# Statistics of a convolution output: separate moments per tile, or sums over the mirrored sum and difference

## The chip, the cores and the metric

The kernel runs on one core of a Trainium2 chip. The metric is the device time in microseconds (us) of one execution, as the median of several runs. A core has five engines that run their own instruction queues in order and wait for each other by semaphores: PE (TensorE, matrix products into PSUM), DVE (VectorE, element-wise work and reductions), ACT (ScalarE, functions of one element with an optional sum over the row), POOL (GpSimd) and SP (which only issues DMA transfers here).

## The reference

The input x has 16 images of 16 channels of 256 x 256 fp32 values. Two layers follow each other, each of the form x + layer(groupnorm(x)). The first layer is a circular 3 x 3 convolution, which the reference writes as a product in the Fourier domain. The second is a Laplace layer (poles and residues in the Fourier domain). What matters here is the normalization between them, called `_gn`: 8 groups of two channels, and for each image and group one mean and one variance over 2 x 256 x 256 values.

```
def _gn(v, G=8, eps=1e-5):
    g = v.reshape(B_, G, C_ // G, H_, W_)
    m = jnp.mean(g, axis=(2, 3, 4), keepdims=True)
    s = jnp.var(g, axis=(2, 3, 4), keepdims=True)
    return ((g - m) / jnp.sqrt(s + eps)).reshape(v.shape)

x = x + _L0_conv_ref(_gn(x), L0_conv_weight)      # the result is v below
x = x + _L1_conv_ref(_gn(x), ...)                 # needs mean and variance of v
```

So every element of v, the output of the first layer, has to enter a sum and a sum of squares before the second layer can scale it.

## The kernel before, in words

The kernel has four stages one after the other: the convolution (up to about 626 us), the transform of the rows and columns (`fold`, `lines`, `columns`), the mixing of channels, and the way back. Only the first stage is touched.

**Tiling.** An image enters as two halves (tiles `xt`, loaded by SP in one DMA each), with 128 partitions that hold four groups r of 32: r = 0, 1 are rows from the top, r = 2, 3 the mirrored rows from the bottom, so that element (row, column) of a tile of r = 0, 1 has its mirror image at the same place of a tile of r = 2, 3. An image makes four units u; the stage has 64 units in all. A unit of one r is a PSUM bank of 128 x 512 values; six banks rotate (`pc`, bufs=6).

**Steps.** The stage is one loop over steps g = 0 to 386, `conv(g)` being the first thing of each. A unit takes six steps of 16 matmul calls (L249), two phases by three taps; r = 2, 3 run three steps behind r = 0, 1. With n = g mod 6, the banks of r = 0, 1 are full at n = 5 and those of r = 2, 3 at n = 2. At once ACT evicts them (L266) into SBUF tiles `vt`, adding the bias. Two steps later (the list `later`) DVE calls `mirror`: it adds the tiles of r = 0, 1 and r = 2, 3 into `vsum` (L231) and subtracts them in place (L232). One step on (the list `folded`) SP gets four stores into the DRAM array vD (L292). The pools set how far this runs ahead: four `vt` tiles, two `vsum` tiles.

**Statistics of v, before.** A unit has four tiles of 512 values per partition. For r = 0 DVE computes mean and variance with bn_stats (L268, into `vst`), two steps after the eviction. For r = 1, 2, 3 the eviction itself also leaves the sum over the row (`accum_out` into `sums`), and a Square on ACT with the bias -mu (L274, into a `junk` tile that nobody reads) leaves the sum of squares about mu, an estimate of the mean of the image. Once per image bn_aggr (L286, and L836 for the last image) joins the four bn_stats. `v_stats` joins both kinds of moments with weights 1 and 3; it runs once for the first 12 images inside the stage, and once for the last four at the start of the next stage.

**What else stands in the queues.** `x_stats(b)` computes the statistics of the input image b some 40 steps ahead: 16 bn_stats of 128 x 512 on DVE (L166), bn_aggr (L174), then small DVE pieces and matmuls of one column in turn (L178 on PE after L174; L186 to L188 on DVE; L178 again; L194; a square root on ACT at L195; L154 to L211; L178; L217 and L218). Every piece has a fixed step before the image begins (22, 17, 16, 14, 12, 9, 5 and 3 steps). The generators of `tables` add pieces of the second layer's tables every second and every fourth step: POOL arithmetic (L497 to L502, L516, L518, L575 to L599), DVE (L508 to L512, reciprocals at L431, L580, L597), ACT functions with table loads (L425, L426, L498, L514) and PE (L450, L612). The order on every engine is the order in which the loop issues (`manual_schedule`): an instruction that waits holds all that stand behind it on its engine.

Of the kernel before, what the change touches and what calls it, by code (L numbers as in the profile page):

```python
# [9 lines left out]
FP = mybir.dt.float32  # L10
AF = mybir.ActivationFunctionType
ALU = mybir.AluOpType
AX = mybir.AxisListType
# [3 lines left out]
B = 16  # L17
C = 16
N = 256
P = 128  # L20
# [4 lines left out]
def conv_then_laplace_kernel(ctx: ExitStack, tc: tile.TileContext, a: dict, out: bass.AP):  # L25
# [15 lines left out]
    nc = tc.nc  # L41
    x = a["x"]
# [45 lines left out]
    tp = ptab.enter_context(tc.tile_pool(name="tables", bufs=1))  # L88
# [70 lines left out]
    def x_stats(b):  # L159


        st = sp.tile([P, C, 6], FP, name="xst", tag="xst")

        def moments(j):
            r0 = 1 + 2 * (j % 8)
            nc.vector.bn_stats(st[:, j, :], halves[b][j // 8][:, r0 : r0 + 2, 1 : N + 1])  # L166

        for j in range(8):
            yield 38 - j, lambda: moments(j)
        for j in range(8, C):  # L170
            yield 30 - j // 2, lambda: moments(j)
        q = sp.tile([P, 12], FP, name="xq", tag="xq")
        mean, pvar, mu, d, e, var, sd, tmp, r, nb, bias = (q[:, j : j + 1] for j in range(11))
        yield 22, lambda: nc.vector.bn_aggr(q[:, 0:2], st)  # L174

        def spread(lhs, rhs):
            ps = pst.tile([P, 512], FP, name="ps_stat", tag="ps_stat")
            nc.tensor.matmul(ps[:, 0:1], lhsT=lhs, rhs=rhs, start=True, stop=True)  # L178
            return ps[:, 0:1]

        ps = []
        yield 17, lambda: ps.append(spread(g128, mean))

        def about_mean():

            nc.vector.tensor_copy(mu, ps[0])  # L186
            nc.vector.tensor_tensor(d, mean, mu, ALU.subtract)
            nc.vector.scalar_tensor_tensor(e, d, d, pvar, ALU.mult, ALU.add)  # L188

        yield 16, about_mean  # L190
        yield 14, lambda: ps.append(spread(g128, e))

        def root():
            nc.vector.tensor_scalar(var, ps[1], 1e-5, None, ALU.add)  # L194
            nc.scalar.activation(sd, var, AF.Sqrt)  # L195

        yield 12, root
        wc = sp.tile([P, 2, 3, 32], FP, name="wc", tag="wc")

        def conv_weights():  # L200
            newton(sd, var, tmp)
            nc.vector.reciprocal(r, sd)
            nc.vector.scalar_tensor_tensor(
                wc.rearrange("p h t m -> p (h t m)"),
                wband.rearrange("p h t m -> p (h t m)"),
                r,
                imask.rearrange("p h t m -> p (h t m)"),
                ALU.mult,
                ALU.add,
            )  # L210
            nc.vector.tensor_scalar(nb, mu, r, -1.0, ALU.mult, ALU.mult)  # L211

        yield 9, conv_weights
        yield 5, lambda: ps.append(spread(wsum.rearrange("p c m -> p (c m)"), nb))

        def biases():
            nc.vector.tensor_copy(bias, ps[2])  # L217
            nc.vector.tensor_scalar(shift[:, b : b + 1], mu, -1.0, None, ALU.mult)  # L218
            ready[b] = wc, bias

        yield 3, biases

    vst = tp.tile([P, B, 4, 6], FP, name="vst", tag="vst")
    sums = tp.tile([P, 2, B, 12], FP, name="sums", tag="sums")
    shift = tp.tile([P, B], FP, name="shift", tag="shift")

    def mirror(g, b, u, lo, hi):
        both = fp.tile([P, 2, 2, N], FP, name="vsum", tag="vsum")  # L230
        nc.vector.tensor_tensor(both, lo, hi, ALU.add)  # L231
        nc.vector.tensor_tensor(lo, lo, hi, ALU.subtract)  # L232
        folded.append((g + 3, b, u, (both, lo)))

    def conv(g):


        for c in range(4):
            for r in range(4):
                at = g if r < 2 else g - 3  # L240
                if not 0 <= at < 24 * B:
                    continue
                b, u, n = at // 24, at // 6 % 4, at % 6
                phase, tap = n // 3, n % 3
                if n == 0 and c == 0:
                    acc[r] = pc.tile([P, 2, N], FP, name="ps_conv", tag="ps_conv")
                q = 8 * (u % 2) + c + phase + (r < 2)
                rows = slice(32 * r, 32 * r + 32)
                nc.tensor.matmul(  # L249
                    acc[r][32 * c : 32 * c + 32],  # L250
                    lhsT=ready[b][0][rows, phase, tap],
                    rhs=halves[b][u // 2][rows, q : q + 5 : 4, 2 - tap : 2 - tap + N],
                    start=n == 0,
                    stop=n == 5,
                )
        for r in (0, 1) if g % 6 == 5 else (2, 3) if g % 6 == 2 else ():
            at = g if r < 2 else g - 3
            if not 0 <= at < 24 * B:
                continue
            b, u = at // 24, at // 6 % 4  # L260
            if r % 2 == 0:
                vt = vp.tile([P, 2, 2, N], FP, name="vt", tag="vt")
                acc["v", r // 2] = vt
            col = slice(3 * u + r - 1, 3 * u + r)
            by_sums = {"accum_out": sums[:, 0, b, col]} if r else {}
            nc.scalar.activation(vt[:, r % 2], acc[r], AF.Identity, bias=ready[b][1], **by_sums)  # L266
            if r == 0:
                later.append((g + 2, lambda b=b, u=u, v=vt[:, 0]: nc.vector.bn_stats(vst[:, b, u], v)))  # L268
            if r % 2 == 0:
                continue  # L270
            for k in (1,) if r == 1 else (2, 3):
                col = slice(3 * u + k - 1, 3 * u + k)
                junk = jp.tile([P, 2, N], FP, name="junk", tag="junk")
                nc.scalar.activation(  # L274
                    junk,
                    vt[:, k % 2],
                    AF.Square,
                    bias=shift[:, b : b + 1],
                    accum_out=sums[:, 1, b, col],
                )  # L280
            if r == 3:
                later.append((g + 2, lambda g=g, b=b, u=u, lo=acc["v", 0], hi=vt: mirror(g, b, u, lo, hi)))
        while later and (later[0][0] <= g or g >= 24 * B + 2):
            later.pop(0)[1]()
        if g % 24 == 4 and g >= 24:
            nc.vector.bn_aggr(ms[:, g // 24 - 1], vst[:, g // 24 - 1])  # L286
        while folded and (folded[0][0] <= g or g >= 24 * B + 2):
            _, b, u, tiles = folded.pop(0)
            for j, t in enumerate(tiles):
                for r in range(2):  # L290
                    y = 64 * r + 16 * u
                    nc.sync.dma_start(  # L292
                        out=vD[b][j, y : y + 16].rearrange("(t y) c x -> (y c) t x", t=2),
                        in_=t[:, r],
                    )

    ms = tp.tile([P, B, 2], FP, name="ms", tag="ms")
    vs = tp.tile([P, 6, B], FP, name="vs", tag="vs")
    vrhs = tp.tile([P, 2, B, C], FP, name="vrhs", tag="vrhs")

    def v_stats(b0, b1, bank):

        bs, nb = slice(b0, b1), b1 - b0
        n = 12.0 * 512
        m1, v1 = ms[:, bs, 0], ms[:, bs, 1]
        m2, v2, d, mean, mu, e = (vs[:, j, bs] for j in range(6))
        tt, ts, st = (
            nc.vector.tensor_tensor,
            nc.vector.tensor_scalar,
            nc.vector.scalar_tensor_tensor,  # L310
        )
        nc.vector.tensor_reduce(m2, sums[:, 0, bs], AX.X, ALU.add)
        nc.vector.tensor_reduce(v2, sums[:, 1, bs], AX.X, ALU.add)
        ts(m2, m2, 1 / n, None, ALU.mult)
        tt(d, m2, shift[:, bs], ALU.add)
        tt(d, d, d, ALU.mult)
        st(v2, v2, 1 / n, d, ALU.mult, ALU.subtract)
        st(mean, m2, 3.0, m1, ALU.mult, ALU.add)
        ts(mean, mean, 0.25, None, ALU.mult)
        yield  # L320
        ps = bank()[:, 0:nb]
        nc.tensor.matmul(ps, lhsT=g128, rhs=mean, start=True, stop=True)
        yield
        nc.vector.tensor_copy(mu, ps)
        for m, v in ((m1, v1), (m2, v2)):
            tt(d, m, mu, ALU.subtract)
            tt(d, d, d, ALU.mult)
            tt(v, v, d, ALU.add)
        st(e, v2, 3.0, v1, ALU.mult, ALU.add)
        ts(e, e, 0.25, None, ALU.mult)  # L330
        r = vrhs[:, :, bs]
        shape = [P, nb, C]
        for j, z in enumerate((mean, e)):
# [295 lines left out]
        for gen in gens:  # L629
            yield from gen  # L630

    ready, acc, later, folded = {}, {}, [], []
    for j, (_, piece) in enumerate(x_stats(0)):
        if j == 8:
            sum_taps()
# [13 lines left out]
    for g in range(24 * B + 3):  # L649
# [3 lines left out]
        b, n = divmod(g, 24)  # L653
# [179 lines left out]
    vq = fold(*units[0], loaded.pop(0))  # L833
    nc.vector.memset(sgn[:, 0:1], -1.0)
    nc.vector.memset(sgn[:, 1:2], 1.0)
    nc.vector.bn_aggr(ms[:, B - 1], vst[:, B - 1])  # L836
    rest = v_stats(B - 4, B, lambda: pa.tile([P, 512], FP, name="ps_y", tag="ps_y"))
    last = None
    for u in range(len(units) + 1):
# [46 lines left out]
    tp = pool(p2, "ct")  # L886
# [596 lines left out]
```

## Time and profile before

| | |
|---|---|
| runs | 2765.16, 2767.58, 2779.18 us; median 2767.58 us |
| profiled execution, first to last instruction | 2764.9 us |
| busy in the whole span | PE 2610.2, DVE 1916.6, ACT 1523.6, POOL 1062.1 us |
| first matmul and last matmul of the convolution | 26.2 and 625.1 us |
| bn_stats of v on DVE (L268) | 64 instructions, 42.9 us |
| Squares on ACT (L274) and their reads | 192 instructions, 138.3 us, and 36.3 us |
| sum (L231) and difference (L232) on DVE | 64 each, 81.0 and 89.0 us |

The profile is of one execution. A group's "busy" is the time covered by its instructions and "mean" the duration of one; two instructions of a pipelined engine can overlap, so a mean can be longer than the pace. "Idle before" is the time in which the engine stood still just before them, and the name after the arrow is what ended it. The chain of waits follows the work that ended last back to its beginning, at each step to what released it.

### The profile page before, as it was taken

To read this page: it belongs to the slowest core of one execution; us is meant where nothing else is said; L and a number is where in the kernel's file an instruction comes from. 1 tells how busy PE (TensorE), PEld (TensorE's weight loads), DVE (VectorE), ACT (ScalarE), POOL (GpSimd) and SP (SyncE) were. 2 spreads that over 40 slices of the span, in tenths; PEclk is the share of its full clock that TensorE was granted. 3 is DMA by queue.
4 is the path that set the end of the run, shared out by engine and by line. 5 is a ranking of instruction groups with operands and counts; after the bars stand their busy time and mean duration, and the time that the engine had idled before them with its cause. 6 is when DMAs were issued, how large, how long until landed. Compare 5 with 4: busy or idle time off the path is not lost.

```text
span 2764.9 us, 93061 instructions
## 1 busy us (share of the span) xinstructions
PE 2610.2 (94%) x39600; PEld 1959.1 (71%) x39600; DVE 1916.6 (69%) x3574; ACT 1523.6 (55%) x3092; POOL 1062.1 (38%) x989
## 2 busy tenths in 40 slices
PE   6888798898999999998999999999989999999998
PEld 3344344456777777776788888888778888888887
DVE  7788799977888888886444444444346667676766
ACT  4667687775666666664455555555434444444443
POOL 1334475612333333334111111111175656565653
PEclk9999999899999999999999999999999999999999
DMA  8778687755566555664666666666699989999995
GB/s 304 250 259 270 221 304 272 252 202 178 207 244 229 213 207 206 244 244 150 194 191 195 189 195 188 197 192 193 201 291 289 288 286 288 288 288 284 288 285 181
DMA packets 481199, 652.82 MB, mean 236 GB/s; under 512 B 51384, under 2 KB 459960, under 8 KB 466832
## 3 DMA queue, kind: packets, MB, share of 16 engines
q1 hardware_dynamic: 479712, 639.65, 71.2%
q8 instruction: 312, 5.11, 0.7%
q0 software_dynamic: 928, 3.02, 0.4%
q10 hardware_dynamic: 144, 4.19, 0.4%
q14 instruction: 103, 0.84, 0.1%
HBM read 367.22 MB, written 279.50 MB: 234 GB/s over the span
## 4 chain that ended last, share of the span: by engine, by line
PE 65%; DVE 13%; DMA 9%; POOL 4%; issue 4%; ACT 2%; SPq 2%; DVEq 0%; ACTq 0%; POOLq 0%
PE ps_mix L1055 16%; PE ps_s L989 9%; PE ps_y L737 8%; PE ps_y L745 8%; PE ps_conv L249 4%; PE ps_x L780 4%; DMA yk<-yD 4%; PE ps_p L1239 4%; PE ps_f L1263 4%; PE ps_f L1264 4%; DMA out_y<-ol 3%; DVE r L1272 2%; DVE xst L166 2%; PE psd L765 1%; DVE ol L1274 1%
## 5 line engine op out<-in xcount | busy, mean ns | idle before, releaser
L1055 PEld LDWEIGHTS ps_mix<-abd,sg 128*64 128x64 f32 x8192 | 447.6, 138 | 59.9 <-ACT sg L1112 48.9
L1055 PE MATMUL ps_mix<-abd,sg 128*64 128x128 f32 x8192 | 478.5, 275 | 7.8 <-ACT yt L1117 7.8
L249 PE MATMUL ps_conv<-xt,wc 32*32 32x512 f32 x12288 | 456.5, 622 | 17.7 <-issue 11.3
L1203 POOL TENSOR_TENSOR u<-yk 128x512 f32<-128x512 f32 (+1 forms) x268 | 343.9, 1314 | 311.0 <-PE ps_p L1239 204.2
L753 ACT ACTIVATE t<-ps_y,vmr 128x384 f32<-128x384 f32 x512 | 297.6, 582 | 163.0 <-PE ps_y L745 162.9
L249 PEld LDWEIGHTS ps_conv<-xt,wc 32*32 32x32 f32 x12288 | 233.0, 105 | 191.3 <-issue 111.9
L1117 DVE COPY yt<-ps_mix 128x512 f32<-128x512 f32 x128 | 88.5, 692 | 357.3 <-PE ps_mix L1055 234.0
L960 POOL TENSOR_TENSOR w<-v,mcol 128x2048 f32<-128x2048 f32 x32 | 115.6, 3612 | 561.5 <-DVE v L949 540.8
L737 PE MATMUL ps_y<-tabE,vq 128*128 128x256 f32 x1024 | 313.7, 388 | 8.7 <-DVE vq L726 7.1
L745 PE MATMUL ps_y<-tabO,vq 128*128 128x256 f32 x1024 | 306.4, 381 | 0.0
L1263 PE MATMUL ps_f<-pt,inv 128*128 128x256 f32 x1008 | 300.4, 380 | 0.0
L1264 PE MATMUL ps_f<-hs,ey 128*128 128x256 f32 x1008 | 299.8, 379 | 0.0
L1117 ACT COPY yt<-ps_mix 128x512 f32<-128x512 f32 x384 | 219.8, 588 | 144.7 <-PE ps_mix L1055 88.2
L1239 PEld LDWEIGHTS ps_p<-inv,u 128*128 128x128 f32 x2048 | 266.1, 193 | 43.2 <-issue 24.7
L1239 PE MATMUL ps_p<-inv,u 128*128 128x128 f32 x2048 | 279.4, 280 | 6.6 <-POOL u L1207 6.5
L1267 DVE TENSOR_TENSOR r<-ps_f,q 128x256 f32<-128x256 f32 x256 | 107.3, 419 | 248.9 <-ACT q L1266 248.9
L989 PE MATMUL ps_s<-ct,w 64*32 64x256 f32 x8448 | 261.0, 381 | 13.1 <-POOL w L957 12.2
L1112 ACT COPY sg<-ps_s 128x512 f32<-128x512 f32 x248 | 159.7, 645 | 190.4 <-PE ps_s L989 190.2
L1266 ACT COPY q<-ps_f 128x256 f32<-128x256 f32 x256 | 95.4, 373 | 285.4 <-PE ps_f L1264 283.1
L737 PEld LDWEIGHTS ps_y<-tabE,vq 128*128 128x128 f32 x1024 | 189.9, 191 | 85.3 <-ACT q L793 50.3
L266 ACT ACTIVATE vt<-ps_conv,xq 128x512 f32<-128x512 f32 x256 | 167.1, 680 | 137.7 <-PE ps_conv L249 135.9
L1241 ACT COPY pt<-ps_p 128x512 f32<-128x512 f32 x256 | 150.2, 587 | 132.4 <-PE ps_p L1239 118.7
(240 smaller groups left out, 4156.9 us busy)
## 6 DMA issues: line engine op xcount, KB each, us to landing
xt<-in_x SPq DMA_DIRECT2D x31, 2322.0 KB, 9.3
abd<-aD SPq DMA_DIRECT2D x512, 128.0 KB, 2.8
yD<-yt SPq DMA_DIRECT2D x512, 128.0 KB, 2.4
vl<-vD SPq DMA_DIRECT2D x256, 256.0 KB, 4.0
out_y<-ol SPq DMA_DIRECT2D x128, 512.0 KB, 9.4
s<-vD SPq DMA_DIRECT2D x252, 256.0 KB, 6.5
aD<-spec SPq DMA_DIRECT2D x15, 4096.0 KB, 12.6
yk<-yD SPq DMA_DIRECT2D x60, 1024.0 KB, 8.5
```

Of the source, the lines that this page charges most:

```text
L249: nc.tensor.matmul(acc[r][32 * c : 32 * c + 32], lhsT=ready[b][0][rows, phase, tap], rhs=halves[b][u // 2][rows, q : q + 5 : 4, 2 - tap : ...
L266: nc.scalar.activation(vt[:, r % 2], acc[r], AF.Identity, bias=ready[b][1], **by_sums)
L737: nc.tensor.matmul(ps[:, 0:N], lhsT=vf[:, xo, 0, j], rhs=tabE[:, 0 : i + 2 : i + 1], start=True, stop=False, skip_group_check=True,)
L745: nc.tensor.matmul(ps[:, P : P + N], lhsT=vf[:, xo, 1, j], rhs=tabO[:, i : C + 1 : C - i], start=False, stop=True, skip_group_check=True,)
L753: nc.scalar.activation(t[:, xo, j].rearrange("p l n -> p (l n)"), ps[:, 0:384], AF.Copy, scale=vmr[:, 0, b0 + j, i : i + 1],)
L989: nc.tensor.matmul(ps[odd][32 * iq : 32 * iq + 32, ro], lhsT=w[rows, iq, kk, ro], rhs=ct[rows, iq, kk], start=True, stop=True,)
L1055: nc.tensor.matmul(ps[64 * t : 64 * t + 64, j], lhsT=sg[:, f : f + 2].rearrange("p f m -> p (f m)"), rhs=abd[jq][:, :, 2 * t + cc, 2 * jj ...
L1117: (nc.vector.tensor_copy if m == 3 else nc.scalar.copy)(o, src)
L1203: nc.gpsimd.tensor_tensor(u[:, :, j].rearrange("p b (c n) -> p c b n", c=8), in0, in1, o)
L1239: nc.tensor.matmul(ps[:, at], lhsT=u[:, n], rhs=tab, start=True, stop=True)
L1263: nc.tensor.matmul(ps[:, e], lhsT=tab, rhs=pt[:, e], start=True, stop=False)
L1264: nc.tensor.matmul(ps[:, e], lhsT=ey[:, e], rhs=hs, start=False, stop=True)
```

## The change

The statistics of v are taken from the two mirrored tiles in place of the four tiles before. With a + b the sum and a - b the difference of mirrored values, the row sum of a + b is the sum of all values, and (a + b - 2 mu)^2 + (a - b)^2 is twice (a - mu)^2 + (b - mu)^2.

- The add of `mirror` becomes a scalar_tensor_tensor (lo x 1 + hi) with an accumulator output, on DVE.
- ACT squares `vsum` with the bias -2 mu, 1024 elements, one step after the stores are issued, and the difference without bias one step later, both with an accumulator output. A new list `squared` holds them; they come after `later` and before `folded` in a step.
- The bn_stats and bn_aggr of v, the accumulator outputs of the evictions and the Squares of 512 elements are gone.
- `biases` computes -2 mu too; `v_stats` has one kind of moments and fewer small instructions; `junk` grows from 512 to 1024 elements.

```diff
@@ x_stats, biases
             nc.vector.tensor_scalar(shift[:, b : b + 1], mu, -1.0, None, ALU.mult)
+            nc.vector.tensor_scalar(shift2[:, b : b + 1], mu, -2.0, None, ALU.mult)
...
     def mirror(g, b, u, lo, hi):
         both = fp.tile([P, 2, 2, N], FP, name="vsum", tag="vsum")
-        nc.vector.tensor_tensor(both, lo, hi, ALU.add)
+        nc.vector.scalar_tensor_tensor(
+            both, lo, 1.0, hi, ALU.mult, ALU.add, accum_out=sums[:, b, u : u + 1]
+        )
         nc.vector.tensor_tensor(lo, lo, hi, ALU.subtract)
         folded.append((g + 3, b, u, (both, lo)))
+        squared.append((g + 4, lambda: square(both, 4 + 2 * u, b, bias=shift2[:, b : b + 1])))
+        squared.append((g + 5, lambda: square(lo, 5 + 2 * u, b)))
+
+    def square(t, col, b, **by):
+
+        junk = jp.tile([P, 4 * N], FP, name="junk", tag="junk")
+        nc.scalar.activation(
+            junk,
+            t.rearrange("p r j x -> p (r j x)"),
+            AF.Square,
+            accum_out=sums[:, b, col : col + 1],
+            **by,
+        )
...
@@ conv
-            col = slice(3 * u + r - 1, 3 * u + r)
-            by_sums = {"accum_out": sums[:, 0, b, col]} if r else {}
-            nc.scalar.activation(vt[:, r % 2], acc[r], AF.Identity, bias=ready[b][1], **by_sums)
-            if r == 0:
-                later.append((g + 2, lambda b=b, u=u, v=vt[:, 0]: nc.vector.bn_stats(vst[:, b, u], v)))
-            if r % 2 == 0:
-                continue
-            for k in (1,) if r == 1 else (2, 3):
-                col = slice(3 * u + k - 1, 3 * u + k)
-                junk = jp.tile([P, 2, N], FP, name="junk", tag="junk")
-                nc.scalar.activation(
-                    junk,
-                    vt[:, k % 2],
-                    AF.Square,
-                    bias=shift[:, b : b + 1],
-                    accum_out=sums[:, 1, b, col],
-                )
+            nc.scalar.activation(vt[:, r % 2], acc[r], AF.Identity, bias=ready[b][1])
             if r == 3:
                 later.append((g + 2, lambda g=g, b=b, u=u, lo=acc["v", 0], hi=vt: mirror(g, b, u, lo, hi)))
...
-        if g % 24 == 4 and g >= 24:
-            nc.vector.bn_aggr(ms[:, g // 24 - 1], vst[:, g // 24 - 1])
+        while squared and (squared[0][0] <= g or g >= 24 * B + 2):
+            squared.pop(0)[1]()
...
@@ v_stats
-        nc.vector.tensor_reduce(m2, sums[:, 0, bs], AX.X, ALU.add)
-        nc.vector.tensor_reduce(v2, sums[:, 1, bs], AX.X, ALU.add)
...
-        st(mean, m2, 3.0, m1, ALU.mult, ALU.add)
-        ts(mean, mean, 0.25, None, ALU.mult)
+        nc.vector.tensor_reduce(mean, sums[:, bs, 0:4], AX.X, ALU.add)
+        nc.vector.tensor_reduce(v2, sums[:, bs, 4:12], AX.X, ALU.add)
...
+        st(v2, v2, 0.5 / n, d, ALU.mult, ALU.subtract)
...
-        for m, v in ((m1, v1), (m2, v2)):
-            tt(d, m, mu, ALU.subtract)
-            tt(d, d, d, ALU.mult)
-            tt(v, v, d, ALU.add)
-        st(e, v2, 3.0, v1, ALU.mult, ALU.add)
-        ts(e, e, 0.25, None, ALU.mult)
+        tt(d, mean, mu, ALU.subtract)
+        tt(d, d, d, ALU.mult)
+        tt(e, v2, d, ALU.add)
...
-    nc.vector.bn_aggr(ms[:, B - 1], vst[:, B - 1])
```

More of the change, by code (lines that the diff above doesn't have):

```diff
@@ L218, in biases @@
             nc.vector.tensor_scalar(shift[:, b : b + 1], mu, -1.0, None, ALU.mult)
+            nc.vector.tensor_scalar(shift2[:, b : b + 1], mu, -2.0, None, ALU.mult)
             ready[b] = wc, bias
         yield 3, biases
-    vst = tp.tile([P, B, 4, 6], FP, name="vst", tag="vst")
-    sums = tp.tile([P, 2, B, 12], FP, name="sums", tag="sums")
+    sums = tp.tile([P, B, 12], FP, name="sums", tag="sums")
     shift = tp.tile([P, B], FP, name="shift", tag="shift")
+    shift2 = tp.tile([P, B], FP, name="shift2", tag="shift2")
     def mirror(g, b, u, lo, hi):
         both = fp.tile([P, 2, 2, N], FP, name="vsum", tag="vsum")
-        nc.vector.tensor_tensor(both, lo, hi, ALU.add)
+        nc.vector.scalar_tensor_tensor(
+            both, lo, 1.0, hi, ALU.mult, ALU.add, accum_out=sums[:, b, u : u + 1]
+        )
         nc.vector.tensor_tensor(lo, lo, hi, ALU.subtract)
         folded.append((g + 3, b, u, (both, lo)))
+        squared.append((g + 4, lambda: square(both, 4 + 2 * u, b, bias=shift2[:, b : b + 1])))
[9 more added lines that the diff above has]
+        )
     def conv(g):
@@ L295, in conv @@
                     )
-    ms = tp.tile([P, B, 2], FP, name="ms", tag="ms")
-    vs = tp.tile([P, 6, B], FP, name="vs", tag="vs")
+    vs = tp.tile([P, 5, B], FP, name="vs", tag="vs")
     vrhs = tp.tile([P, 2, B, C], FP, name="vrhs", tag="vrhs")
@@ L303, in v_stats @@
         bs, nb = slice(b0, b1), b1 - b0
-        n = 12.0 * 512
-        m1, v1 = ms[:, bs, 0], ms[:, bs, 1]
-        m2, v2, d, mean, mu, e = (vs[:, j, bs] for j in range(6))
+        n = 16.0 * 512
+        v2, d, mean, mu, e = (vs[:, j, bs] for j in range(5))
         tt, ts, st = (
@@ L311, in v_stats @@
         )
-        nc.vector.tensor_reduce(m2, sums[:, 0, bs], AX.X, ALU.add)
-        nc.vector.tensor_reduce(v2, sums[:, 1, bs], AX.X, ALU.add)
-        ts(m2, m2, 1 / n, None, ALU.mult)
-        tt(d, m2, shift[:, bs], ALU.add)
+        nc.vector.tensor_reduce(mean, sums[:, bs, 0:4], AX.X, ALU.add)
+        nc.vector.tensor_reduce(v2, sums[:, bs, 4:12], AX.X, ALU.add)
+        ts(mean, mean, 1 / n, None, ALU.mult)
+        tt(d, mean, shift[:, bs], ALU.add)
         tt(d, d, d, ALU.mult)
-        st(v2, v2, 1 / n, d, ALU.mult, ALU.subtract)
-        st(mean, m2, 3.0, m1, ALU.mult, ALU.add)
-        ts(mean, mean, 0.25, None, ALU.mult)
+        st(v2, v2, 0.5 / n, d, ALU.mult, ALU.subtract)
         yield
@@ L630, in chain @@
             yield from gen
-    ready, acc, later, folded = {}, {}, [], []
+    ready, acc, later, folded, squared = {}, {}, [], [], []
     for j, (_, piece) in enumerate(x_stats(0)):
```

## The prediction

> **What bounds the kernel now.** I read the windows first, to see which stretch of the span the change can touch. The columns are the window, then busy us and instruction count of PE, PEld, DVE, ACT and POOL, then the TensorE clock and the DMA.
>
> ```profile
> core 0: us, PE busy (x) PEld busy (x) DVE busy (x) ACT busy (x) POOL busy (x), PEclk, DMA share, GB/s
> 0.00:26.00 26.00, 1.52 (x6) 1.35 (x6) 13.90 (x37) 1.49 (x2) 0.19 (x4) 1.00 0.86 333
> 26.00:200.00 174.00, 148.93 (x3338) 72.84 (x3337) 142.36 (x252) 117.16 (x260) 61.60 (x49) 0.93 0.79 265
> 200.00:350.00 150.00, 126.04 (x2956) 62.20 (x2956) 123.30 (x208) 104.05 (x232) 67.67 (x57) 0.96 0.71 244
> 350.00:500.00 150.00, 135.13 (x3549) 69.11 (x3527) 143.06 (x221) 125.09 (x297) 97.34 (x101) 0.98 0.82 292
> 500.00:600.00 100.00, 86.29 (x2160) 45.14 (x2156) 88.56 (x172) 66.94 (x165) 38.65 (x43) 0.91 0.60 215
> 600.00:626.00 26.00, 25.72 (x760) 17.80 (x741) 12.43 (x13) 20.99 (x55) 3.17 (x4) 1.00 0.66 223
> ```
>
> The convolution runs from 26 to 626 us. DVE is busy 142.4 + 123.3 + 143.1 + 88.6 + 12.4 = 510 of those 600 us, PE 522, ACT 434. From 350 to 500 DVE is full (95%). Before that neither PE nor DVE is: they wait for each other. After 600 PE alone sets the pace: the last units follow each other every 6.2 us, against 600/64 = 9.4 us on average.
>
> Next, who waits for whom inside that stretch (us, times, longest), and the groups of DVE and of ACT that the change touches, from 0 to 640 us (busy us, mean ns, idle before and who ended it):
>
> ```profile
> ACT vt L266 <- PE ps_conv L249: 135.9, 58, 12.1
> ...
> DVE vsum L231 <- ACT vt L266: 31.5, 14, 3.3
> ...
> PE ps_stat L178 <- DVE xq L188: 26.1, 9, 6.6
> PEld ps_conv L249 <- ACT vt L266: 19.4, 24, 5.9
> ```
>
> ```profile
> L232 DVE TENSOR_TENSOR vt<-vt 128x1024 f32<-128x1024 f32 x64 | 89.0, 1390 | 2.2
> L231 DVE TENSOR_TENSOR vsum<-vt 128x1024 f32<-128x1024 f32 x64 | 81.0, 1265 | 34.2 <-ACT vt L266 34.2
> L268 DVE BATCH_NORM_STATS2 vst<-vt 128x6 f32<-128x512 f32 x64 | 42.9, 670 | 5.9 <-ACT vt L266 5.9
> ...
> L286 DVE BATCH_NORM_AGGREGATE ms<-vst 128x2 f32<-128x24 f32 x15 | 3.8, 252 | 0.0
> ```
>
> ```profile
> L266 ACT ACTIVATE vt<-ps_conv,xq 128x512 f32<-128x512 f32 x256 | 167.1, 680 | 137.7 <-PE ps_conv L249 135.9
> L274 ACT ACTIVATE junk<-vt,shift 128x512 f32<-128x512 f32 x192 | 138.3, 720 | 4.2
> L266 ACT ACTIVATION_READ_ACCUMULATOR vt<-ps_conv,xq 128x1 f32 x192 | 37.7, 197 | 0.0
> L274 ACT ACTIVATION_READ_ACCUMULATOR junk<-vt,shift 128x1 f32 x192 | 36.3, 189 | 0.0
> ```
>
> PE's largest wait is for the statistics of the next image (xq, L188), which DVE delivers late because other work stands ahead of them in its queue. ACT has slack: it waits 136 us for PE. So a DVE instruction less is worth something, an ACT instruction less little. The chain of waits from 26 to 626 us, added up piece by piece, has 177 us of DVE, 160 of PE, 94 of POOL, 60 of ACT, 22 of DMA and 86 of "issue". On it lie 21 of the 64 vst instructions (12.4 us), 22 of the vsum ones (27.3 us), 4 of ms (0.7 us), and 37.6 us of evictions and squares (L266 26.4, L274 11.2).
>
> **What the Trainium skill says.** "ScalarE: Activation LUTs", What ACT_TABLE_LOAD costs: an ACTIVATE takes about 186 ns + 0.833 ns per element, 93 ns more with a per-partition bias. The trace agrees: L274, with bias, 720 ns for 512; L425 with a per-partition operand 714 and L426 without 620. "VectorE: DVE Perf Modes", Two Vector instructions with no wait between them: an op that also writes its accumulator is two instructions, the second an accumulator read. The trace of before shows no such DVE op; on ACT the pair is there (L266, L274). "Vector Engine (DVE) Microarchitecture Reference", Points that are easy to get wrong: a scalar_tensor_tensor with two non-bf16 SBUF sources halves throughput, with no port left for accumulator readback. Without accumulator the trace disagrees: L1272, two fp32 SBUF sources, takes 2321 ns for 2048, the rate of a tensor_tensor (1219 ns for 1024 in L729). With one, no row shows it.
>
> **The change part by part.**
>
> 1. DVE, removed: 64 vst at 670 ns = 42.9 us, 16 ms at 0.25 us = 4.1 us. Both stand in the in-order queue in front of the xq pieces: at image step 24b-17 a vst comes directly ahead of L186 to L188. On the chain: -12.4 - 0.7 = -13.1 us.
> 2. DVE, the sum becomes a scalar_tensor_tensor with accumulator. The element rate is that of L1272, so the main part stays at 1218 ns. Unknown is the accumulator read. Lower bound: nearly nothing, as on ACT, where in back-to-back pairs the read lengthens the pace by 0.10 us though it lasts 0.19. Upper bound: half rate. From L725 (512 elements, 693 ns) to L729 (1024, 1219 ns) an element costs 1.03 ns, so 1024 more are 1.05 us. A cost below zero is excluded: same elements, one write more. I take 0.15 us, a small DVE instruction (L186 lasts 0.14). 64 x 0.15 = 9.6 us of work, 22 x 0.15 = +3.3 us on the chain. Its two SBUF inputs are those of the old add, so nothing changes against POOL.
> 3. DVE, one shift2 per image: 16 x 0.142 (L218) = 2.3 us, times DVE's share of the chain (177/600) = +0.7 us. v_stats loses 7 small instructions per call (0.17 to 0.6 us each); one call lies behind the chain's xq pieces at 504 us, the other is on the chain at 642 us: -1 us in all.
> 4. ACT, per unit before: four evictions at a pace of 0.575 us, three reads at 0.095, three squares at 0.84 with read = 5.1 us. After: four evictions 2.3; a square of 1024 with bias 720 + 512 x 0.833 = 1146 ns and one without 1053 ns, each with 0.12 for the read: 2.44; 4.74 in all. Saving 7% of ACT's 37.6 us on the chain: -2.7 us. Evictions also end 0.1 to 0.2 us earlier. There is no change in table loads (47 either way).
> 5. ACT, the new wait. The squares of unit k stand behind the evictions of r 0, 1 of unit k+1 and wait for DVE's sum and difference; queued behind them are the evictions of r 2, 3 of unit k+1, and the square roots and table pieces of the other generators. Unit by unit: the difference (L232) ends a median 0.3 us after those evictions, but 3 us or more in 15 units. With 0.5 us less DVE lag and 1.17 us of square after it, the next eviction would start later than now in 35 units, more than 2.2 us later in 5. PE needs the bank three steps (3.5 us) after it was filled and the pair takes 1.27 us to evict, so 2.2 us are covered by the six banks; the 5 units exceed this by 5.9 us together. Half of that was PE waiting anyway: +3 us. What is late next there is the eviction, then PE's first matmul of the next r 2, 3 group.
> 6. DMA: the same four stores per unit at the same step on SP's queue. The tiles are freed by the stores; the squares, one and two steps after the issue, end about when the store lands (2.1 to 9 us after its issue). Nothing: the next user of a vsum buffer is the sum two units, 12 steps, later; only with that cover gone would a square (1.2 us) hold DVE or an eviction.
> 7. "Issue" pieces of the chain hide a stretch (434 to 482 us, 28 us) in which POOL waits for ACT, and ACT for DVE at full load: 28 x (35 us saved of 510) = -2 us.
>
> Sum: -13.1 + 3.3 + 0.7 - 1 - 2.7 + 3 - 2 = -11.8 us. The profiled span of 2764.9 us becomes 2753; it stands 2.7 us under the median of the runs shown, 2767.6, which becomes 2756. The removed pieces bound the gain of this one chain; PE and POOL chains lie close behind it, so I count no second-order gain.
>
> **The rivals.** *DVE is the bound everywhere:* then all of its saving counts, 42.9 + 4.1 - 9.6 - 2.3 = 35 us, less the PE-bound tail: about 30 us, 2737. For it: 95% from 350 to 500. Against it: 82% before that, and 48 us in which DVE waits for ACT (L231, L268, xq L174).
>
> *Another path takes over:* the POOL chain of the tables (94 us on the chain, L497 to L502 ahead of L508) or the new wait of step 5 in full (+6) eat the gain: 2763 to 2768. For it: PE, DVE, ACT and POOL take turns on the chain. Against it: the vst sits in front of the very xq pieces that PE waits for longest.
>
> *Slower, the accumulator at half rate:* the sum takes 2.3 us instead of 1.22. On the chain 22 x 1.05 = 23 us instead of 3.3 gives +8; by DVE's total, 64 x 1.05 = 67 against 45 us removed, +22, and the mirror's delay lands on the ACT squares of step 5 as well. 2775 to 2795, say 2784. It decides from 0.7 us of extra per sum (45 us/64). For it: the skill's sentence. Against it: L1272 shows no halving. *The change doing less than it says* is no case: the instruction lists show vst, ms and the 192 small squares gone.
>
> **How the numbers follow.** A measurement of this kernel can tell about 0.5% (14 us) from no change. The forecast (5 to 20 us faster) has 0.45, of which 0.2 is beyond 14 us; DVE as the bound everywhere 0.13; another path takes over (within 5 us) 0.24; half rate 0.18, all but 0.01 slower by over 14 us if counted with a bad case of step 5. That gives 0.33 faster, 0.50 within, 0.17 slower. The likeliest time is 2756 (own range 2747 to 2763); the range that takes in the others is 2735 to 2785.
>
> **What would show it.** Right: vsum at 1.2 to 1.3 us with a read of 0.1 to 0.2, squares at about 1.15 and 1.05 us, the stretch from 26 to 626 us some 10 us shorter, the PE wait for xq L188 below 26 us, and a new ACT wait for vsum or vt of some tens of us that PE hardly feels. Wrong: vsum at 2.3 us (half rate); PE waits for vt well over 20 us (step 5 too small); or an unchanged stage end with more POOL and PE on the chain.

## The result and the profile after

Twelve runs of each kernel gave medians of 2761.8 us (after) and 2772.1 us (before). The ratio of all runs is 0.9965, with a 95% interval of 0.995 to 0.998: about 10 us faster (6 to 14). That is less than the half per cent at which the prediction put the limit of what can be told, but the interval leaves out 1. A second measurement of the same kernel, in the last group of experiments, gave 0.9953 (0.9938 to 0.9969), 13 us. The median of before is here 4.5 us above that of the three runs that the prediction started from (2767.6), so it is the difference that can be compared with the forecast, not the 2756 us.

The profile of after is of the fastest of its twelve executions (2749.86 us). The profile of its second measurement is of the slowest of six (2765.85 us); in it the stage ends at 614.5 us and PE waits 12.5 us for xq L188. What the two traces of one kernel differ by (609.2 against 614.5 us, 10.1 against 12.5 us) is what a single trace can't tell.

The windows of the kernel after, in the columns of the prediction's first fence:

```profile
26.00:200.00 174.00, 150.99 (x3437) 73.47 (x3437) 139.65 (x258) 114.02 (x181) 63.46 (x51) 0.93 0.82 273
200.00:350.00 150.00, 133.90 (x3061) 61.22 (x3061) 117.12 (x215) 101.52 (x168) 73.71 (x65) 0.98 0.76 254
350.00:500.00 150.00, 139.53 (x3560) 67.19 (x3554) 137.98 (x239) 118.80 (x204) 97.04 (x97) 1.00 0.83 290
500.00:600.00 100.00, 90.43 (x2459) 51.31 (x2459) 73.14 (x144) 69.26 (x125) 37.03 (x41) 0.97 0.63 220
```

PE does more in every window: 150.99 against 148.93, 133.90 against 126.04, 139.53 against 135.13, 90.43 against 86.29. The last convolution matmul ends at 609.2 us instead of 625.7. The whole stage, in the kernel before and then in the kernel after:

```profile
26.00:625.70 599.70, 522.09 (x12704) 267.10 (x12703) 509.71 (x863) 433.96 (x1006) 268.43 (x252) 0.95 0.74 256
26.00:609.00 583.00, 523.84 (x12703) 258.44 (x12703) 471.05 (x856) 410.03 (x686) 271.69 (x252) 0.97 0.78 263
```

What gets shorter is the idle time of PE, from 77.6 to 59.2 us. The granted clock rises with the change, from 0.95 to 0.97, but PE's busy time does not fall (522 and 524 us), so the gain does not show as faster matmuls. Added up over the convolution, DVE's busy time falls by 38.7 us (509.7 to 471.1) but the stage by 16.5, so most of what DVE saves turns into idle time of DVE: 90 us of it before, 112 after.

The waits of the kernel after inside the stage (us in total, times, longest):

```profile
ACT vt L280 <- PE ps_conv L265: 114.8, 59, 11.1
...
DVE vsum L232 <- ACT vt L280: 47.0, 24, 4.1
ACT junk L243 <- DVE vsum L232: 43.0, 17, 7.3
...
PEld ps_conv L265 <- ACT vt L280: 25.8, 30, 6.8
...
PE ps_stat L178 <- DVE xq L188: 10.1, 4, 5.8
...
PE ps_conv L265 <- ACT vt L280: 8.8, 8, 5.8
```

PE's wait for evictions on the matmuls, in before:

```profile
PE ps_conv L249 <- ACT vt L266: 6.3, 4, 5.0
```

This is the trade. PE's wait for the next image's statistics (xq L188) falls from 26.1 to 10.1 us. The new wait, ACT for DVE's sum, is there with 43 us. PE's waits for evictions grow (19.4 to 25.8 on the weight loads, 6.3 to 8.8 on the matmuls), and DVE waits more for evictions (31.5 to 47.0).

The touched groups of DVE and of ACT (busy, mean ns, idle before):

```profile
L235 DVE TENSOR_TENSOR vt<-vt 128x1024 f32<-128x1024 f32 x64 | 89.3, 1395 | 2.2
L232 DVE SCALAR_TENSOR_TENSOR vsum<-vt 128x1024 f32<-128x1024 f32 x64 | 80.4, 1256 | 51.8 <-ACT vt L280 47.0 <-DMA s<-vD 4.8
...
L232 DVE DVE_READ_ACCUMULATOR vsum<-vt 128x1 f32 x64 | 5.1, 80 | 0.0
```

```profile
L280 ACT ACTIVATE vt<-ps_conv,xq 128x512 f32<-128x512 f32 x256 | 160.3, 681 | 115.3 <-PE ps_conv L265 114.8
L243 ACT ACTIVATE junk<-vsum,shift 128x1024 f32<-128x1024 f32 x64 | 73.3, 1146 | 43.3 <-DVE vsum L232 43.0
L243 ACT ACTIVATE junk<-vt 128x1024 f32<-128x1024 f32 x64 | 67.7, 1057 | 4.4 <-DVE vt L235 2.9
```

The sum with accumulator runs at the rate of the plain add (1256 against 1265 ns), and its read takes 80 ns. The squares are as worked out (1146 and 1057 ns). Where the new wait stands in the queue shows in the timeline of one unit (start, duration, what):

```profile
141.13 1.26 ACT L280 ACTIVATE vt<-ps_conv,xq 128x512 f32<-128x512 f32 x2 [2.02 <-PE ps_conv L265]
...
143.04 1.22 DVE L232 SCALAR_TENSOR_TENSOR vsum<-vt 128x1024 f32<-128x1024 f32 x1
144.18 0.08 DVE L232 DVE_READ_ACCUMULATOR vsum<-vt 128x1 f32 x1
...
144.30 1.23 DVE L235 TENSOR_TENSOR vt<-vt 128x1024 f32<-128x1024 f32 x1
144.30 1.15 ACT L243 ACTIVATE junk<-vsum,shift 128x1024 f32<-128x1024 f32 x1 [1.90 <-DVE vsum L232]
...
145.62 1.06 ACT L243 ACTIVATE junk<-vt 128x1024 f32<-128x1024 f32 x1
...
146.68 1.24 ACT L280 ACTIVATE vt<-ps_conv,xq 128x512 f32<-128x512 f32 x2
```

The accumulator read begins before the sum has ended, and the difference starts 1.26 us after the sum, where the plain add of before took 1.24 (407.51 to 408.75 us in its trace). Over all 64 units the medians of this step are 1.27 and 1.25 us. ACT, after the evictions at 141.13, stands still for 1.9 us; the next evictions start at once after the second square, with no idle time in front: what they needed was there before ACT came to them.

### The profile page after: what moved, and what is told of

The parts are those of the page before. It is cut to its first block, busy times and chain, and to the rows that moved or that the text cites. A ratio compares the mean times of both kernels' runs of the same rounds, so it can differ in the third digit from the quotient of the medians.

```text
span 2748.0 us, 92740 instructions
## 1 busy us (share of the span) xinstructions
PE 2611.5 (95%) x39600; PEld 1950.7 (71%) x39600; DVE 1875.8 (68%) x3560; ACT 1497.9 (55%) x2772; POOL 1068.9 (39%) x989
## 4 chain that ended last, share of the span: by engine, by line
PE 68%; DVE 11%; DMA 8%; POOL 5%; issue 4%; ACT 2%; SPq 2%; DVEq 0%; ACTq 0%; POOLq 0%
PE ps_mix L1047 16%; PE ps_s L981 9%; PE ps_y L730 9%; PE ps_y L738 8%; PE ps_p L1231 5%; PE ps_f L1255 4%; PE ps_x L773 4%; PE ps_f L1256 4%; PE ps_conv L265 4%; DMA yk<-yD 4%; DVE r L1264 2%; DVE xst L166 2%; DMA out_y<-ol 2%; PE psd L758 1%; PE ps_h L1215 1%
## 5 line engine op out<-in xcount | busy, mean ns | idle before, releaser
L265 PE MATMUL ps_conv<-xt,wc 32*32 32x512 f32 x12288 | 462.4, 614 | 25.3 <-issue 16.1
L265 PEld LDWEIGHTS ps_conv<-xt,wc 32*32 32x32 f32 x12288 | 225.7, 104 | 212.9 <-issue 128.7
L981 PE MATMUL ps_s<-ct,w 64*32 64x256 f32 x8448 | 261.7, 382 | 12.4 <-POOL w L949 12.2
L280 ACT ACTIVATE vt<-ps_conv,xq 128x512 f32<-128x512 f32 x256 | 160.3, 681 | 115.3 <-PE ps_conv L265 114.8
## 6 DMA issues: line engine op xcount, KB each, us to landing
aD<-spec SPq DMA_DIRECT2D x15, 4096.0 KB, 12.5
```

What stands on the lines that cost most here:

```text
L265: nc.tensor.matmul(acc[r][32 * c : 32 * c + 32], lhsT=ready[b][0][rows, phase, tap], rhs=halves[b][u // 2][rows, q : q + 5 : 4, 2 - tap : ...
L981: nc.tensor.matmul(ps[odd][32 * iq : 32 * iq + 32, ro], lhsT=w[rows, iq, kk, ro], rhs=ct[rows, iq, kk], start=True, stop=True,)
```

## The experiments

Theory 1 is that of the prediction: DVE work that stands in front of the xq pieces delays PE, and ACT is mostly covered. Theory 2 is that ACT's relief brings the gain, theory 3 that the POOL and ACT chain of the tables bounds the stage. All ratios are against the kernel before, measured in the same group; 0.001 is 2.8 us. The groups are the first measurement of after; a_no_vst, e_vst_back, b_no_squares and d_late_squares; f_squares_of_hi, g_vst_twice, c_no_accum and h_late_half; and the last four. Kernels measured in two groups differ by 0.0012 (after), 0.0014 (late squares) and 0.0031 (late and halved), so a comparison across groups is good to some 3 to 9 us. "End of stage" is the end of the last convolution matmul in the one profiled execution.

| kernel | ratio (95%) | end of stage | PE for xq L188 | PE and PEld for evictions |
|---|---|---|---|---|
| before | 1 | 625.7 | 26.1 | 6.3 and 19.4 |
| after | 0.9965 (0.995 to 0.998) | 609.2 | 10.1 | 8.8 and 25.8 |
| a_no_vst | 0.996 (0.9946 to 0.9975) | 615.8 | 11.3 | 5.3 and 14.5 |
| e_vst_back | 1.0001 (0.9988 to 1.0013) | 626.4 | 25.2 | 11.6 and 29.7 |
| b_no_squares | 0.9915 (0.9899 to 0.9931) | 598.3 | 10.4 | 2.1 and 6.9 |
| d_late_squares | 0.9944 (0.9926 to 0.9962) | 610.2 | 11.6 | 3.7 and 14.0 |
| f_squares_of_hi | 0.9971 (0.9961 to 0.9981) | 620.5 | 12.4 | 18.1 and 41.2 |
| g_vst_twice | 1.0128 (1.011 to 1.0146) | 646.6 | 24.5 | 5.7 and 17.9 |
| c_no_accum | 0.9952 (0.9936 to 0.9969) | 614.3 | 13.7 | 11.3 and 30.9 |
| h_late_half | 0.9896 (0.9878 to 0.9914) | 609.8 | 9.2 | 3.9 and 9.6 |

**One part alone: the bn_stats out of the kernel before** (a_no_vst).

```diff
-                later.append((g + 2, lambda b=b, u=u, v=vt[:, 0]: nc.vector.bn_stats(vst[:, b, u], v)))
...
-            nc.vector.bn_aggr(ms[:, g // 24 - 1], vst[:, g // 24 - 1])
...
+    nc.vector.memset(ms, 1.0)
```

> The kernel before without its 64 bn_stats and 16 bn_aggr of v (the tiles of r = 0 are left out of the statistics of v; a constant stands for their moments). Theory 1 (the gain comes from DVE, whose queue holds up the statistics of the next image): all of steps 1 is realised here and nothing of the ACT changes, so 12 to 18 us faster than before, near 2757 us, ratio about 0.995, and the PE wait for xq L188 falls from 26 us to near 10 us. Theory 2 (the gain comes from ACT: no accumulator reads in the evictions, squares moved): no change here, ratio 1.000. Theory 3 (the POOL and ACT chain of the tables is what bounds the stage): less than 5 us, ratio 0.998 to 1.000.

0.996, 11 us (7 to 15): theory 1, if a little below its 12 to 18 us. The wait for xq L188 falls with ACT as before:

```profile
PE ps_stat L178 <- DVE xq L188: 11.3, 6, 3.9
```

Theory 2 expected no change and falls, and so does theory 3, which expected less than 5 us.

**The part undone: the bn_stats back in the kernel after** (e_vst_back).

```diff
+            if r == 0:
+                later.append((g + 2, lambda b=b, u=u, v=vt[:, 0]: nc.vector.bn_stats(vst[:, b, u], v)))
...
+            nc.vector.bn_aggr(ms[:, g // 24 - 1], vst[:, g // 24 - 1])
```

> The kernel after with the 64 bn_stats and 15 of the bn_aggr of v put back at their old places, their results unused. Theory 1: the gain is gone; step 2 and 3 (accumulator read, shift2) and the new ACT wait remain, so 0 to 8 us slower than before, ratio 1.000 to 1.003, and the PE wait for xq L188 is back at 20 us or more. Theory 2: it keeps the gain of after, ratio about 0.9965. Theory 3: between, 0.997 to 0.999.

1.0001: the whole gain is gone, and the wait for xq L188 is back:

```profile
PE ps_stat L178 <- DVE xq L188: 25.2, 9, 6.6
```

So the gain is the 64 bn_stats and their aggregates (15 of the 16 are back here), and everything else in the change (accumulator, squares, shift2, new wait) nets to nothing within 0.13%, some 3.5 us either way.

**No squares on ACT** (b_no_squares).

```diff
-        squared.append((g + 4, lambda: square(both, 4 + 2 * u, b, bias=shift2[:, b : b + 1])))
-        squared.append((g + 5, lambda: square(lo, 5 + 2 * u, b)))
...
+    nc.vector.memset(sums, 2048.0)
```

> The kernel after without the two squares per unit on ACT (the sums of squares of v are a constant). It takes away 2.4 us per unit of ACT work and the new wait of ACT for DVE. If the new wait costs PE what step 5 said (+3 us) and ACT work is worth its share of the chain (2.44 of 4.74 us on some 35 us, 15 to 18 us), it is about 15 to 20 us faster than after, near 2744, ratio about 0.990. If ACT is covered by its slack, within 5 us of after (ratio 0.995 to 0.998). If the new wait is the larger part of what was lost, more than 20 us faster than after, ratio below 0.989.

0.9915, 14 us below the first measurement of after and 11 below the second. ACT is not fully covered: the squares, with their place and their wait, cost 11 to 14 us, a little less than the 15 to 20 that were expected.

**Squares behind the evictions** (d_late_squares).

```diff
-        squared.append((g + 4, lambda: square(both, 4 + 2 * u, b, bias=shift2[:, b : b + 1])))
-        squared.append((g + 5, lambda: square(lo, 5 + 2 * u, b)))
+        squared.append((g + 6, lambda: square(both, 4 + 2 * u, b, bias=shift2[:, b : b + 1])))
+        squared.append((g + 7, lambda: square(lo, 5 + 2 * u, b)))
```

> The kernel after with both squares two steps later, so that they stand behind the evictions of r 2, 3 of the next unit instead of ahead of them. The ACT wait for vsum (43 us in after) should fall below 10 us and PE's wait for evictions (8.8 us, and 25.8 us for weight loads) to the level of before. If the new wait costs time (step 5: +3 us): 2 to 5 us faster than after, ratio 0.994 to 0.996. If ACT's wait for DVE is only slack spent: the same as after, 0.9965. If the evictions of r 0, 1 then come late instead (mirror waits for squares): slower than after, 0.998 to 1.000.

0.9944. The interval overlaps that of after, so it was repeated (below). ACT's wait for vsum is nearly gone, and PE's weight loads wait less for evictions than before the change:

```profile
PEld ps_conv L265 <- ACT vt L280: 14.0, 21, 4.5
...
ACT junk L243 <- DVE vsum L232: 1.7, 1, 1.7
```

**The wait alone: squares of the tiles of r = 2, 3** (f_squares_of_hi).

```diff
-        squared.append((g + 4, lambda: square(both, 4 + 2 * u, b, bias=shift2[:, b : b + 1])))
-        squared.append((g + 5, lambda: square(lo, 5 + 2 * u, b)))
+        squared.append((g + 4, lambda: square(hi, 4 + 2 * u, b, bias=shift2[:, b : b + 1])))
+        squared.append((g + 5, lambda: square(hi, 5 + 2 * u, b)))
```

> The kernel after with the two squares per unit, at the same places of the ACT queue and of the same size, taken of the tiles of r = 2, 3, which ACT itself evicted long before: the ACT work of after without its wait for DVE (the sums of squares are then not those of v). If the new wait costs what the late squares gave back (after 0.9965, late squares 0.9944, without squares 0.9915), this run lies with the late squares, ratio 0.994 to 0.995, and the rest down to 0.9915 (8 us) is the price of the work itself. If the place of the squares ahead of the evictions is what costs and not the wait, it stays with after, 0.9965. If the wait is all that squares cost, 0.992.

0.9971: nothing gained by taking the wait of the squares for DVE away, and the stage ends later (620.5 us) than in either trace of after. What ACT waits for in this kernel shows why:

```profile
ACT vt L280 <- PE ps_conv L265: 126.4, 55, 11.3
ACT vt L280 <- DMA vD<-vt: 28.4, 11, 4.8
```

No square waits for DVE any more, but 28 us of waits stand in front of the evictions instead, for the stores of a `vt` tile, and these stores are issued only after DVE's difference. So in this run the four `vt` tiles tie ACT to DVE even so, and the wait of the squares seems to be largely one that would have come one eviction later. Since the edit puts one wait in the place of another, it does not isolate the price of the wait, nor show what share of the cost is the squares' time ahead of the evictions and what the stores'.

**The removed cost doubled** (g_vst_twice).

```diff
-                later.append((g + 2, lambda b=b, u=u, v=vt[:, 0]: nc.vector.bn_stats(vst[:, b, u], v)))
+                later.append((g + 2, lambda b=b, u=u, v=vt[:, 0]: [nc.vector.bn_stats(t[:, b, u], v) for t in (vst, vst2)]))
```

> The kernel before with every bn_stats of v done twice, the second into a tile that nobody reads: 64 x 0.67 = 43 us more DVE work at the place where the change removed it. Theory 1 (removed DVE work is paid at about a quarter, 11 us of 47): the same or a higher price for adding it, since DVE has less idle time left, 11 to 25 us slower than before, ratio 1.004 to 1.009, the PE wait for xq L188 well over 26 us. The rival that DVE is the bound everywhere: 35 to 43 us slower, 1.013 to 1.016. Theory 3 (tables of POOL and ACT): below 1.003.

1.0128, 35 us for 38 us of added DVE time (L269, busy 80.8 against 42.9 us). By the total this looks like a DVE bound everywhere. But the convolution is only 21 us longer (646.6 against 625.7), 0.55 us per us added, which is inside the forecast of theory 1. The other sign that it named, a wait for xq L188 well over 26 us, did not come. That wait and the whole stage in g_vst_twice:

```profile
PE ps_stat L178 <- DVE xq L188: 24.5, 8, 5.6
```

```profile
26.00:646.60 620.60, 533.73 (x12703) 269.88 (x12702) 546.12 (x927) 434.31 (x1007) 270.02 (x252) 0.93 0.72 248
```

PE's idle time grows by 9 us (77.6 to 86.9) and its busy time by 12 (522.1 to 533.7), at a granted clock of 0.93 against 0.95. So the added DVE work is not paid at xq L188, and about half of it not as idle time of PE. Whether the lower clock is the cause of the longer busy time, no run separates.

The rest of the loss comes at the start of the mixing stage, which the edit does not touch. Of before and then of g_vst_twice, the mixing matmuls with their first and last start, the issue of the load `ct` that they need, and a wait of DVE for the load queued behind it:

```profile
L1055 PE MATMUL ps_mix<-abd,sg x8192: 272/273/477, 1288.1 to 1999.2; 128*64 128x128 f32 x200
1232.89 0.33 SPq L904 DMA_DIRECT2D ct<-cD  x1
```

```profile
L1056 PE MATMUL ps_mix<-abd,sg x8192: 272/273/474, 1326.7 to 2040.3; 128*64 128x128 f32 x200
1274.62 0.33 SPq L905 DMA_DIRECT2D ct<-cD  x1
DVE prU L919 <- DMA p2k<-in_pole_k: 18.9, 1, 18.9
```

The mixing matmuls take about as long as before (714 and 711 us from first to last), but they begin 55.4 us after the last matmul of the transform (`ps_y`) instead of 37.6. In g_vst_twice `ct` is issued 3 us after that matmul ends (1271.3 us); in the thirteen other kernels, before (1250.5 us) and after among them, 17 to 18 us ahead of its end. So of the 41 us between the two traces (2805.9 and 2764.9 us), 21 lie in the convolution and 18 are a late load at the start of the mixing stage. All five runs of this kernel lie between 2806 and 2816 us, so it is not one odd execution. The issue of `ct` waited 20.2 us for a matmul of `ps_x`, which it does not wait for in before. This kernel has a tile in the convolution that before lacks (`vst2`), so a shifted placement in memory is a likely reason; no run shows it.

**Without accumulator** (c_no_accum).

```diff
-        nc.vector.scalar_tensor_tensor(
-            both, lo, 1.0, hi, ALU.mult, ALU.add, accum_out=sums[:, b, u : u + 1]
-        )
+        nc.vector.tensor_tensor(both, lo, hi, ALU.add)
...
+    nc.vector.memset(sums, 0.0)
```

> The kernel after with the sum of mirror as the plain tensor_tensor add of before, without accumulator (the mean of v is then a constant 0). It takes away 64 accumulator reads of 80 ns, 5.1 us of DVE, and nothing else. Theory 1: a quarter to a third of that, 1 to 2 us faster than after, ratio 0.9955 to 0.9965, not told from after. If the accumulator form costs more than its duration shows (a pause before the next instruction): 4 us or more, ratio below 0.995.

0.9952, just below the second measurement of after (0.9953) and with an interval that takes in both: the accumulator form has no price that can be told. Half rate, which the prediction put at 23 us on the chain, is excluded twice, here and by the 1256 ns.

**Late and halved squares** (h_late_half).

```diff
-            nc.vector.tensor_scalar(shift2[:, b : b + 1], mu, -2.0, None, ALU.mult)
...
-        squared.append((g + 4, lambda: square(both, 4 + 2 * u, b, bias=shift2[:, b : b + 1])))
-        squared.append((g + 5, lambda: square(lo, 5 + 2 * u, b)))
+        squared.append((g + 6, lambda: square(both, 4 + 2 * u, b, bias=shift[:, b : b + 1])))
+        squared.append((g + 7, lambda: square(lo, 5 + 2 * u, b)))
...
             AF.Square,
+            scale=0.5,
...
```

> The kernel after with both squares two steps later and computed as (0.5 (a + b) - mu)^2 and (0.5 (a - b))^2, so that the bias -mu of before serves and the 16 small DVE instructions for -2 mu are gone (2.3 us of DVE). Theory 1 gives these a quarter of their time, below 1 us: the same as with late squares alone, ratio 0.994, about 2757 us. If small pieces in the xq sequence count in full: 0.9935.

0.9896, 13 us better than late squares alone for 2.3 us of DVE less. None of the theories explains that, so the last four kernels ran together as a square: place of the squares by form of the bias.

> The kernel after once more, as one corner of a square of four kernels that run together: squares ahead of or behind the evictions of r 2, 3, and -2 mu computed by 16 small DVE instructions or saved by halving. It should repeat 0.9965 within 0.0015.

> The late squares once more. If the place of the squares is worth 5 us: 0.002 below after2 (0.9945). If the first measurement was chance: equal to after2 within 0.001.

> The kernel after with the squares halved in place of the 16 small DVE instructions for -2 mu, at their early places. If the 13 us between late squares and late halved squares come from these instructions: 0.005 below after2, about 0.9915. By theory 1 (2.3 us of DVE, paid at a quarter to four fifths): less than 2 us, 0.996.

> Late and halved squares once more. Theory 1: like d2_late within 2 us, 0.9935 to 0.9945, and the 0.9896 of the first time was largely chance of the later stages, which differ by some 10 us between executions. If it repeats 0.990, both edits together do something that neither does alone.

| | bias -2 mu on DVE | halved squares |
|---|---|---|
| ahead of the evictions | after2 0.9953 (0.9938 to 0.9969) | i_half 0.9961 (0.9947 to 0.9975) |
| behind them | d2_late 0.993 (0.9915 to 0.9946) | h2_late_half 0.9927 (0.9906 to 0.9947) |

The place is worth 0.0023 and 0.0034 (6 and 9 us) in the two columns, and 0.0021 in the first measurement. Each pair alone is at the edge of its intervals; together the twelve runs with early squares have a mean of 2761.3 us and the twelve with late ones 2753.8. The form of the bias is worth nothing that can be told (+0.0008, -0.0003); the 0.9896 did not repeat. The stage ends of the four agree: 614.5 (after2), 608.8 (d2_late), 612.1 (i_half), 607.6 us (h2_late_half). The first pair of traces, 609.2 (after) and 610.2 (d_late_squares), does not show it. d2_late is the version to keep: 16 and 19 us faster than before in its two measurements.

## Why the prediction was right, point by point

The forecast was 11.8 us faster; 10 (6 to 14) and 13 us (9 to 17) were measured, and in the two profiles the stage ends 16.5 and 11.2 us earlier. The mechanism, DVE work that delays the statistics PE waits for, is the one that the runs show for the work removed. That the sum came so close is in part luck: step 5 was too small by 3 to 6 us, step 2 too large by about 3, and what else is in the sum made up for it: the terms beside step 1 add up to +1.3 us, and e_vst_back shows that they net to nothing within 3.5 us. By its steps:

- **Step 1** (bn_stats and bn_aggr, -13.1 us): shown, by a_no_vst (-11 us) and by e_vst_back, where the gain vanishes with them. Reading the pieces of the chain was a good measure here: 47 us removed, 13 of them on the chain, 11 paid. The wait for xq L188 fits in the kernels without bn_stats (8 to 14 us against 26) and in e_vst_back (25.2), but not in g_vst_twice, where double the work left it at 24.5.
- **Step 2** (accumulator, +3.3 us): mis-sized, as an upper side. I priced the read at 0.15 us on DVE's queue; it lasts 0.08 and overlaps the end of the sum, so that the difference starts 0.02 us later than before. On 22 pieces of the chain that is an estimated 0.4 us. The rival of half rate fell: with an accumulator too, the sentence of the Trainium skill ("Vector Engine (DVE) Microarchitecture Reference", Points that are easy to get wrong: two non-bf16 SBUF sources halve the throughput of a scalar_tensor_tensor) is not what fp32 operands show here against a plain add (1256 ns for 1024 elements, 1265 for the tensor_tensor of before).
- **Step 3** (shift2, +0.7 us, v_stats, -1 us): shift2 costs nothing that the square of four can tell; v_stats was not tested.
- **Steps 4 and 5** (ACT, -2.7 and +3 us): their sum of nothing is shown by e_vst_back (1.0001), together with steps 2 and 3. Step 5 was too small: the place of the squares alone costs 6 to 9 us, not 3. What ACT saves would then have to be larger than 2.7 by about as much; no run measures it alone. I worked step 5 out as a wait for DVE; f_squares_of_hi has no such wait and is no faster, but there the evictions wait for stores instead. So the runs show that the place ahead of the evictions costs, and leave open how much of that is the 2.4 us of squares and how much the tie to DVE through the tiles. "ACT has slack" was also too generous: without squares the kernel is 11 to 14 us faster than after.
- **Step 6** (stores): right for this kernel, whose evictions show no wait for a store. In f_squares_of_hi, where the squares' own wait is gone, they wait 28 us for stores.
- **Step 7** ("issue" pieces, -2 us): no run separates it.

The rivals: DVE as the bound everywhere would have been 30 us; the removed work is paid at about a quarter (11 of 47 us), and added work at 0.55 inside the stage (21 of 38). The other path is there, but only took its share: on the chain of the stage, DVE goes from 177 to 149 us and POOL from 94 to 117.

## What to carry to other kernels

To price a removed instruction on an in-order queue, read how much of it lies on the chain of waits; the busy time saved says little (here 47 us saved, 13 on the chain, 11 paid). When work moves to another engine, look at where it stands in that engine's queue: behind the evictions, which PE needs, the same squares cost 6 to 9 us less than ahead of them. When an experiment costs more than expected, find the stage in which it does: 18 of the 41 us by which the trace of g_vst_twice is longer were a late load in a stage that the edit does not touch. A late stage can vary by 8 us from one execution to the next; two edits measured as a square in one group told 6 to 9 us from nothing, and would not have told one microsecond.

## What the runs showed that I had not expected

- The last stage, from the end of the last mixing matmul to the end, takes 764 to 765 us in three of the profiled executions (before, after, g_vst_twice) and 772 to 773 in nine others, whatever was done to the first stage (767 in i_half, 769 in d2_late). The nine and d2_late have one idle time of PE of 5.0 us near its beginning, for the DVE tile `r`, that the other four lack; why it comes or not is open. With a spread of single runs of after from 2750 to 2769 us, this is why the end of a stage is read beside the total.
- An accumulator read on DVE is almost free in this kernel: 80 ns, begun before the sum ended, 0.02 us in the pace.
- A DVE instruction of one element, L187, took 1.06 us in the trace of after where its mean is 0.27. POOL was in a tensor_tensor of the tables, and both ended at 156.5 us:

```profile
154.61 1.91 POOL L509 TENSOR_TENSOR s_th<-s_th,s_ex 128x512 f32<-128x512 f32 x1 [12.94 <-ACT s_th L507]
...
155.47 1.06 DVE L187 TENSOR_TENSOR xq<-xq 128x1 f32<-128x1 f32 x1
```

  That the one held the other is likely but not shown. Small pieces in a sequence that another engine waits for are not always small.
